# Moving block sums to VectorE and regrouping LN moments, transposes and first-group sums in a fused LayerNorm and graph attention kernel

## The chip, the cores and the metric

The kernel runs on one core of a Trainium2 chip. The metric is the device time of one execution in microseconds (us), the median of several runs. The core has five engines that work side by side, each through its own list of instructions in order: TensorE (in the profile PE, its weight loads PEld), VectorE (DVE), ScalarE (ACT), GpSimd (POOL) and SyncE (SP), which here only starts transfers.

## The reference

x has 128 samples of 128 nodes and 768 features, adj one 128 x 128 matrix for each sample. All is in 32-bit floats.

```
h = max(layernorm(x), 0)                       # over the 768 features
q, k, v = h@Wq + bq, h@Wk + bk, h@Wv + bv      # split into 12 heads of 64
s = q@k^T / 8 + beta * adj;   s = -9e15 where adj == 0
out = x + softmax(s) @ v
```

## The kernel before

Samples are taken in 32 groups of four (NG groups, index G). For each group the normalized input is transposed into six blocks A00 to A12 of 128 x 512 (two sample pairs by three feature blocks). The projections to q, k and v are not done as plain products of blocks: each of three slices of the weights (qk0, v and qk1) is a 3 x 3 arrangement of weight blocks, and a scheme of 15 products of sums of blocks stands in for the 18 products of the plain way. The left factors are the 11 sums of A blocks in SUMS_A (`sum_acts`, called S in the profile) and the right ones the 15 steps of weight sums in SUMS_B (`sum_weights`, T), which are made once, in the first group. The products go into four chains a, b, c and d, each a PSUM bank that TensorE goes on accumulating into; after each product its bank is read out (`product`, L300): the first use of an output goes through an activation on ScalarE or, for v, an add with the bias on VectorE (L325), all later uses are adds on VectorE (L330 for v, L339 for q and k). The next product of a chain has to wait until the bank has been read.

A group goes through slices qk0, v and qk1 in this order (L446 to L490). Between the products of a slice stands other work, listed in `todo` by the number of the product behind which it is written:

- qk0 of group G: the second half of the attention of group G-1, and the loads of x for group G+1.
- v of group G: statistics (`stats`), the mean and variance of group G+1 by two small matmuls (`moments_1`, `moments_2`, PSUM tile pm), its mask (`bias_1`, `bias_2`), and the normalization on ScalarE (`norm`, L256).
- qk1 of group G: the first half of the attention of group G, and the transposes (`to_hT`, L263) and block sums of group G+1.

Attention of a pair of heads is `scores` (matmuls sc, then on VectorE the mask, e, L356, and the exponential on ScalarE, L357) and four products later `attend` (matmuls av, the division on VectorE, the addition to x on GpSimd, xo, L377, and the store). The variance's power -0.5 is on GpSimd (L245).

The first group takes its qk0 slice in the plain way (`plain_slice`), since no weight sums are there yet; `half` normalizes it in two halves, and `after` puts an instruction behind the last transpose and the last GpSimd step of that.

The written order is not quite the order of the engines. A scheduler of the language may move an instruction ahead in its engine's list where nothing that it depends on stands in between; `tc.issue_after(i)` forbids it to stand ahead of instruction i on i's engine. Tiles with `bufs=1` are one buffer: the transposes and sums of group G+1 overwrite those of group G and wait for TensorE's last use of them. The four x tiles of a group are one set of four buffers, so a load of x for the group after next waits for the transposes of the next one.

Before, one in three of the weight sums (n % 3 == 2) and of the activation sums (n % 3 == 1) is on GpSimd, and in the first group all qk0 sums that the choice leaves open:

```
e = e or (nc.gpsimd if n % 3 == 2 else nc.vector)
e.tensor_tensor(wt[sl, name], wt[sl, a], wt[sl, b], ALU.add if sign > 0 else ALU.subtract)
```

Of the kernel before, what the change touches and what calls it, by code (L numbers as in the profile page):

```python
# [104 lines left out]
def direct(ctx, tc, x, adj, wq, bq, wk, bk, wv, bv, beta, out, bad):  # L105
# [82 lines left out]
    def sum_weights(sl, n, e=None):  # L188
        name, a, b, sign = SUMS_B[n]
        if (sl, name) not in wt:  # L190
            raw = [r for r, home in HOME.items() if home == name]
            wt[sl, name] = wt[sl, raw[0]] if raw else const.tile([P, 2, H2], F32, name=f"{sl}_{name}")
        if a[0] == "-":
            nc.vector.scalar_tensor_tensor(wt[sl, name], wt[sl, a[1:]], -1.0, wt[sl, b], op0=ALU.mult,
                                           op1=ALU.add if sign > 0 else ALU.subtract)
        else:
            e = e or (nc.gpsimd if n % 3 == 2 else nc.vector)
            e.tensor_tensor(wt[sl, name], wt[sl, a], wt[sl, b], ALU.add if sign > 0 else ALU.subtract)
# [67 lines left out]
    def sum_acts(G, n):  # L266
        name, a, b, sign = SUMS_A[n]
        t = work.tile([P, 2, H2], F32, tag=name, name=f"{name}_{G}", bufs=1)
        e = nc.gpsimd if n % 3 == 1 else nc.vector
        e.tensor_tensor(t, A[G, a], A[G, b], ALU.add if sign > 0 else ALU.subtract)  # L270
        A[G, name] = t
# [9 lines left out]
    def bias_1(G, raw):  # L281
# [8 lines left out]
        nc.gpsimd.tensor_tensor(a, a, a, ALU.mult)  # L290
# [7 lines left out]
    banks = {}  # L298

    def product(G, sl, n):  # L300
# [15 lines left out]
        for (r, j), sign in uses:  # L316
            key = (G, sl, r, j)
            if sl == "v":
                got = p.rearrange("p g (h d) -> p (g h) d", d=HD)
                if key not in vt:  # L320
# [4 lines left out]
                    nc.vector.tensor_tensor(o4, bias[:, None, :, :].to_broadcast([P, 2, 4, HD]),  # L325
                                            p.rearrange("p g (h d) -> p g h d", d=HD),
                                            ALU.add if sign > 0 else ALU.subtract)
                else:
                    o = vt[key][:, :, 0:HD]
                    nc.vector.tensor_tensor(o, o, got, ALU.add if sign > 0 else ALU.subtract)  # L330
# [6 lines left out]
            else:  # L337
                t = qk[key]
                nc.vector.tensor_tensor(t, t, p, ALU.add if sign > 0 else ALU.subtract)  # L339
# [297 lines left out]
```

## Time and profile before

| | |
|---|---|
| median of 3 runs | 3205.62 us (3204.83 to 3207.76) |
| the profiled execution | 3205.0 us |
| its span, first to last instruction | 3203.1 us |
| mean granted TensorE clock | 0.993 |
| from one V slice to the next, in the middle of the run | 98.05 us |
| first plain slice, from its first matmul | 33.7 us |
| first V slice | 53.04 us |

All views are of one execution. A row of a timeline gives the start, the length, the engine, the line, the operation, what it writes and reads, the count, and in brackets how long the engine was idle before it and what ended that. Rows of one kind that follow one another are merged into one. A row of waits gives the engine that waited, for whom, the total, the count and the longest. A row of stretches gives the stretch, its length and the busy time of each engine in it. Slices in this kernel are read from PE's rows: pc_v with idle or work of another slice ahead is the start of a V slice, pc_qk that of a qk slice.

### The profile page before, as it was taken

To read this page: it belongs to the slowest core of one execution; us is meant where nothing else is said; L and a number is where in the kernel's file an instruction comes from. 1 tells how busy PE (TensorE), PEld (TensorE's weight loads), DVE (VectorE), ACT (ScalarE), POOL (GpSimd) and SP (SyncE) were. 2 spreads that over 40 slices of the span, in tenths; PEclk is the share of its full clock that TensorE was granted. 3 is DMA by queue.
4 is the path that set the end of the run, shared out by engine and by line. 5 is a ranking of instruction groups with operands and counts; after the bars stand their busy time and mean duration, and the time that the engine had idled before them with its cause. 6 is when DMAs were issued, how large, how long until landed. Compare 5 with 4: busy or idle time off the path is not lost.

```text
span 3203.1 us, 46402 instructions
## 1 busy us (share of the span) xinstructions
PE 3115.6 (97%) x17822; PEld 2743.3 (86%) x17822; DVE 1963.9 (61%) x4988; ACT 781.2 (24%) x1665; POOL 590.1 (18%) x489
## 2 busy tenths in 40 slices
PE   5999999999999999999999999999999999999998
PEld 4888888888888888888888888888888888888887
DVE  7665666665565655666655656556666656665554
ACT  1222223222122222232221322222322213222221
POOL 5121111111211111111112111111111111111110
PEclk8999999999999999999999999999999999999998
DMA  5211211111121112212111211112121112121111
GB/s 150 53 50 47 56 54 50 53 47 49 53 60 49 51 43 58 55 50 54 45 52 53 57 50 53 43 55 59 47 56 45 52 53 57 47 57 37 50 40 31
DMA packets 358385, 169.94 MB, mean 53 GB/s; under 512 B 84368, under 2 KB 358032, under 8 KB 358160
## 3 DMA queue, kind: packets, MB, share of 16 engines
q1 hardware_dynamic: 355296, 166.14, 18.9%
q8 instruction: 142, 2.33, 0.3%
q10 hardware_dynamic: 2864, 0.79, 0.1%
q14 instruction: 83, 0.68, 0.1%
HBM read 116.53 MB, written 50.33 MB: 52 GB/s over the span
## 4 chain that ended last, share of the span: by engine, by line
PE 87%; DVE 6%; POOL 3%; issue 2%; ACT 1%; DMA 1%; SPq 1%; ACTq 0%; POOLq 0%; DVEq 0%
PE pc_qk L314 17%; PE pb_qk L314 14%; PE pa_qk L314 14%; PE av L366 10%; PE pd_qk L314 7%; PE sc L353 7%; PE pb_v L314 5%; PE pc_v L314 5%; PE pa_v L314 4%; PE pd_v L314 3%; POOL rstd L245 3%; DVE A L263 2%; DVE v L330 2%; ACT x L256 1%; SPq L180 0%
## 5 line engine op out<-in xcount | busy, mean ns | idle before, releaser
L256 ACT ACTIVATE x<-x,shift,rstd 128x192 f32<-128x192 f32 x512 | 228.0, 533 | 911.7 <-POOL shift L247 911.7
L357 ACT ACTIVATE e<-e 128x512 f32<-128x512 f32 x384 | 235.6, 630 | 821.8 <-DVE e L356 821.8
L377 POOL TENSOR_TENSOR xo<-xo,o 128x512 f32<-128x512 f32 x192 | 244.2, 1272 | 975.0 <-DVE seen L375 590.3
L366 PEld LDWEIGHTS av<-v,e 128*128 128x128 f32 x3072 | 375.6, 193 | 15.4 <-ACT e L357 5.4
L366 PE MATMUL av<-v,e 128*128 128x65 f32 x3072 | 367.2, 273 | 4.7 <-ACT e L357 4.7
L314 PE MATMUL pb_qk<-S,qk_T 128*128 128x256 f32 x1512 | 367.2, 386 | 0.0
L263 DVE STREAM_TRANSPOSE A<-x 128x256 f32<-128x256 f32 x384 | 222.0, 617 | 155.4 <-ACT x L256 120.1
L314 PEld LDWEIGHTS pb_qk<-S,qk_T 128*128 128x128 f32 x1512 | 277.3, 190 | 40.2
L356 DVE SCALAR_TENSOR_TENSOR e<-sc,biasT 128x512 f32<-128x512 f32 x384 | 246.5, 683 | 104.0 <-PE sc L353 103.8
L339 DVE TENSOR_TENSOR qk<-qk,pb_qk 128x512 f32<-128x512 f32 x252 | 171.7, 681 | 175.5 <-PE pb_qk L314 154.5
L335 ACT ACTIVATE qk<-pc_qk,bqk 128x256 f32<-128x256 f32 x378 | 158.3, 470 | 475.4 <-PE pc_qk L314 475.4
L314 PE MATMUL pa_qk<-S,qk_T 128*128 128x256 f32 x1008 | 244.7, 386 | 0.0
L314 PE MATMUL pc_qk<-S,qk_B 128*128 128x256 f32 x1008 | 244.7, 386 | 0.0
L314 PE MATMUL pc_qk<-S,qk_T 128*128 128x256 f32 x1008 | 238.1, 379 | 0.0
L353 PE MATMUL sc<-qk 64*128 64x128 f32 x3072 | 224.4, 285 | 0.0
L314 PEld LDWEIGHTS pc_qk<-S,qk_T 128*128 128x128 f32 x1008 | 191.5, 190 | 26.0
L353 PEld LDWEIGHTS sc<-qk 64*128 64x128 f32 x3072 | 187.1, 188 | 30.1 <-issue 21.2
L314 PEld LDWEIGHTS pc_qk<-S,qk_B 128*128 128x128 f32 x1008 | 186.3, 190 | 30.4
L314 PEld LDWEIGHTS pa_qk<-S,qk_T 128*128 128x128 f32 x1008 | 186.3, 190 | 30.4
L270 POOL TENSOR_TENSOR S<-S,A 128x512 f32<-128x512 f32 x64 | 82.2, 1285 | 630.0 <-PE pa_qk L314 601.1
L339 DVE TENSOR_TENSOR qk<-qk,pd_qk 128x512 f32<-128x512 f32 x126 | 86.6, 687 | 178.1 <-PE pd_qk L314 178.1
L245 POOL TENSOR_TENSOR rstd<-ve,nhalf 128x16 f32<-128x16 f32 (+1 forms) x33 | 93.4, 2830 | 524.6 <-DVE ve L243 524.6
(114 smaller groups left out, 4808.9 us busy)
## 6 DMA issues: line engine op xcount, KB each, us to landing
xo<-in_x_dram SPq DMA_DIRECT2D x192, 256.0 KB, 2.8
out_dram<-xo SPq DMA_DIRECT2D x192, 256.0 KB, 2.2
x<-in_x_dram SPq DMA_DIRECT2D x504, 96.0 KB, 2.2
adj<-in_adj_dram SPq DMA_DIRECT2D x128, 64.0 KB, 2.3
qk_T<-in_L_gnn_Wq_dram SPq DMA_DIRECT2D x10, 128.0 KB, 3.2
qk_T<-in_L_gnn_Wk_dram SPq DMA_DIRECT2D x10, 128.0 KB, 3.3
v_T<-in_L_gnn_Wv_dram SPq DMA_DIRECT2D x5, 256.0 KB, 5.4
qk_B<-in_L_gnn_Wq_dram SPq DMA_DIRECT2D x8, 128.0 KB, 3.4
```

Source lines behind the costliest of these rows:

```text
L245: nc.gpsimd.tensor_tensor(r, ve, nhalf.to_broadcast([P, n]), ALU.pow)
L256: nc.scalar.activation(t, t, AF.Relu, bias=shift[G, n], scale=rstd[G, n])
L263: last = nc.vector.transpose(t[:, :, g * N:(g + 1) * N].rearrange("p c (b i) -> p c b i", i=SQ), src)
L270: e.tensor_tensor(t, A[G, a], A[G, b], ALU.add if sign > 0 else ALU.subtract)
L314: nc.tensor.matmul(p[:, i, :], lhs, rhs, start=(first and i == 0 and c == 0), stop=(c == 1), skip_group_check=True)
L335: nc.scalar.activation(t[:, i, :], p[:, i, :], AF.Identity, bias=bqk[:, i, oc:oc + 1], scale=float(sign))
L339: nc.vector.tensor_tensor(t, t, p, ALU.add if sign > 0 else ALU.subtract)
L353: nc.tensor.matmul(ps[i][:, g, :], t[r, 1, at], t[r, 0, at], start=True, stop=True)
L356: nc.vector.scalar_tensor_tensor(e, ps[i], SCORE_CAP * ISCALE, biasT[G], op0=ALU.min, op1=ALU.add)
L357: nc.scalar.activation(e, e, AF.Exp, scale=1.0 / ISCALE)
L366: nc.tensor.matmul(pa[:, 2 * g + i, :], es[G, oc, i][:, 2 * r + g, :], vt[G, "v", r, h // 4][:, 4 * g + h % 4, :], start=True, stop=True)
L377: nc.gpsimd.tensor_add(t, t, o.rearrange("p a (b j) d -> p (a b) (j d)", j=2))
```

## The change

All block sums go to VectorE, those of weights and those of activations; GpSimd keeps the power, the mask's fill and the addition of x. The mask's square (for a later check of its size) goes from GpSimd to ScalarE. In all groups but the first, statistics of group G+1 are written into the qk0 slice, the moments behind products 1 and 3 of the V slice instead of 5 and 8, and the normalization behind products 6 to 9 instead of 11 to 14; the loads of x are written earlier. The transposes of group G+1 are forbidden to stand ahead of the last V add of group G. In the first group the second half's normalization is written one step earlier; the sums of qk1 and the first mask come into the V slice and must stand behind V's first adds made so far; eight of the qk0 sums follow in the qk1 slice, seven in the next group's qk0 slice.

```
     def sum_weights(sl, n):
...
-            e = e or (nc.gpsimd if n % 3 == 2 else nc.vector)
-            e.tensor_tensor(wt[sl, name], wt[sl, a], wt[sl, b], ALU.add if sign > 0 else ALU.subtract)
+            nc.vector.tensor_tensor(wt[sl, name], wt[sl, a], wt[sl, b], ALU.add if sign > 0 else ALU.subtract)
...
     def sum_acts(G, n):
...
-        e = nc.gpsimd if n % 3 == 1 else nc.vector
-        e.tensor_tensor(t, A[G, a], A[G, b], ALU.add if sign > 0 else ALU.subtract)
+        nc.vector.tensor_tensor(t, A[G, a], A[G, b], ALU.add if sign > 0 else ALU.subtract)
...
     def bias_1(G, raw):
...
-        nc.gpsimd.tensor_tensor(a, a, a, ALU.mult)
+        nc.scalar.activation(a, a, AF.Square)
...
+    def behind_adds(f, *args):
+        with tc.issue_after(added[0].ins):
+            return f(*args)
...
             for g in range(GRP):
-                then(11, lambda g=g: load_x(G + 1, g, (nc.sync,)))
+                then(6, lambda g=g: load_x(G + 1, g, (nc.sync,)))
+                if G:
+                    then(11 + g, lambda g=g: stats(G + 1, g))
...
-            then(3, lambda: half(1, 2))
+            then(2, lambda: half(1, 2))
...
-                then(n // 3 + 13, lambda n=n: after(sum_weights, "qk1", n))
-            then(9, lambda: bias_2(0, after(bias_1, 0, adj_0)))
             plain_slice(0, "qk0", todo)
         else:
+            if G == 1:
+                for n in range(8, len(SUMS_B)):
+                    then(n - 8, lambda n=n: sum_weights("qk0", n))
             slice_of(G, "qk0", todo)
         todo = {}
-        if not G:
-            for n in range(len(SUMS_B)):
-                then(n, lambda n=n: after(sum_weights, "qk0", n, nc.gpsimd))
         if G + 1 < NG:
             got = []
+            at = 1 if G else 6
             for g in range(GRP):
-                then(g, lambda g=g: stats(G + 1, g))
-                then(11 + g, lambda g=g: norm(G + 1, g))
-            then(5, lambda: got.extend(moments_1(G + 1, 0, GRP * NB)))
-            then(7, lambda: got.append(bias_1(G + 1, load_adj(G + 1))))
-            then(8, lambda: moments_2(G + 1, 0, GRP * NB, *got[:2]))
-            then(11, lambda: bias_2(G + 1, got[2]))
+                if not G:
+                    then(g, lambda g=g: stats(G + 1, g))
+                then(at + 5 + g, lambda g=g: norm(G + 1, g))
+            then(at, lambda: got.extend(moments_1(G + 1, 0, GRP * NB)))
+            then(at + 2, lambda: moments_2(G + 1, 0, GRP * NB, *got[:2]))
+            if G:
+                then(8, lambda: got.append(bias_1(G + 1, load_adj(G + 1))))
+                then(12, lambda: bias_2(G + 1, got[2]))
+            else:
+                for n in range(len(SUMS_B)):
+                    then(n, lambda n=n: behind_adds(sum_weights, "qk1", n))
+                then(10, lambda: bias_2(0, behind_adds(bias_1, 0, adj_0)))
         slice_of(G, "v", todo)
         todo = attention(G, 0)
+
+        def transposes(n):
+            with tc.issue_after(added[G].ins):
+                to_hT(G + 1, int(n[1]), int(n[2]))
+
+        if not G:
+            for n in range(8):
+                then(n, lambda n=n: behind_adds(sum_weights, "qk0", n))
+            then(13, lambda: bias_2(1, bias_1(1, load_adj(1))))
         if G + 1 < NG:
             for n, at in HT_AT.items():
-                then(at, lambda n=n: to_hT(G + 1, int(n[1]), int(n[2])))
+                then(at, lambda n=n: transposes(n))
```

`added[G]` is the last add of a product's bank that has been written for group G (in `product`, all three kinds of adds on VectorE set it).

How the instructions stand on the engines is shown at three places. First VectorE at the end of a V slice, that of group 8, before. In the names v0 to v6 are tiles of v, pa_8_v the bank of chain a in the V slice of group 8, and A01_9 a block of group 9.

```order
L330 TENSOR_TENSOR v1_109<-v1_109,pc_8_v_5783 128x8x64
L263 STREAM_TRANSPOSE A01_9_5937<-x_9_0_5721 128x2x128
L263 STREAM_TRANSPOSE A00_9_5966<-x_9_0_5721 128x2x128
L330 TENSOR_TENSOR v4_112<-v4_112,pa_8_v_5794 128x8x64
L263 STREAM_TRANSPOSE A02_9_5985<-x_9_0_5721 128x2x128
L263 STREAM_TRANSPOSE A01_9_5937<-x_9_1_5726 128x2x128
L263 STREAM_TRANSPOSE A00_9_5966<-x_9_1_5726 128x2x128
L330 TENSOR_TENSOR v1_109<-v1_109,pb_8_v_5804 128x8x64
```

The same place in the changed kernel:

```order
L328 TENSOR_TENSOR v1_109<-v1_109,pc_8_v_5800 128x8x64
L328 TENSOR_TENSOR v4_112<-v4_112,pa_8_v_5806 128x8x64
L328 TENSOR_TENSOR v1_109<-v1_109,pb_8_v_5820 128x8x64
L328 TENSOR_TENSOR v3_111<-v3_111,pc_8_v_5800 128x8x64
L328 TENSOR_TENSOR v2_110<-v2_110,pa_8_v_5806 128x8x64
L328 TENSOR_TENSOR v6_114<-v6_114,pb_8_v_5820 128x8x64
L262 STREAM_TRANSPOSE A01_9_5937<-x_9_0_5651 128x2x128
L262 STREAM_TRANSPOSE A01_9_5937<-x_9_1_5656 128x2x128
```

The transposes of group 9 stood among the last adds of V; they now stand behind all of them, and the adds follow one another.

Second VectorE in the first group, at the first adds of its V slice (v0 and v1 with the bias bv_b), before. qk1_T and qk0_T are weight sums of slices qk1 and qk0, and st_1 the statistics of group 1; eight more sums of qk1 stand ahead of the first row.

```order
L198 TENSOR_TENSOR qk1_T13_234<-qk1_T13_234,qk1_B01_231 128x512
L198 TENSOR_TENSOR qk1_T1_462<-qk1_T1_462,qk1_B21_237 128x512
L198 TENSOR_TENSOR qk1_T4_228<-qk1_T10_225,qk1_T4_228 128x512
L194 SCALAR_TENSOR_TENSOR qk0_T9_488<-qk0_B01_131,qk0_B12_143 128x512
L218 BN_STATS st_1_490<-x_1_0_396 128x6 x3
L325 TENSOR_TENSOR v0_108<-bv_b_155,pc_0_v_482 128x8x64
```

The same place in the changed kernel:

```order
L268 TENSOR_TENSOR S11_0_436<-A11_0_300,A01_0_216 128x512
L197 TENSOR_TENSOR qk0_T13_134<-qk0_T13_134,qk0_B01_131 128x512
L217 BN_STATS st_1_455<-x_1_0_333 128x6 x4
L323 TENSOR_TENSOR v0_108<-bv_b_155,pc_0_v_449 128x8x64
L194 SCALAR_TENSOR_TENSOR qk1_T9_460<-qk1_B01_231,qk1_B12_243 128x512
L217 BN_STATS st_1_455<-x_1_1_338 128x6 x2
L323 TENSOR_TENSOR v1_109<-bv_b_155,pa_0_v_462 128x8x64
```

The sums of qk1 stood ahead of the first add; they now begin behind it and lie between the adds. From the first S to that add stand 27 sums, those of the activations and of the V weights and one of qk0.

Third VectorE in the qk1 slice of group 8, around the second pair of e, before. sm, rs, seen and o are the division of `attend`, sc_8_1 the scores of the second pair of heads, S3_9, S6_9 and S8_9 sums for group 9.

```order
L372 TENSOR_TENSOR o_8_0_6007<-av_8_0_1_6020,rs_8_0_1_6027 128x256
L375 TENSOR_TENSOR seen_104<-seen_104,rs_8_0_1_6027 128x4
L356 SCALAR_TENSOR_TENSOR e_8_1_0_6046<-sc_8_1_0_6036,biasT_8_5203 128x512
L356 SCALAR_TENSOR_TENSOR e_8_1_1_6049<-sc_8_1_1_6037,biasT_8_5203 128x512
L270 TENSOR_TENSOR S3_9_6077<-A00_9_5966,A01_9_5937 128x512
```

The same place in the changed kernel:

```order
L370 TENSOR_TENSOR o_8_0_6007<-av_8_0_1_6020,rs_8_0_1_6027 128x256
L373 TENSOR_TENSOR seen_104<-seen_104,sm_8_0_1_6025 128x4
L373 TENSOR_TENSOR seen_104<-seen_104,rs_8_0_1_6027 128x4
L268 TENSOR_TENSOR S8_9_6063<-A10_9_5997,A11_9_5975 128x512
L354 SCALAR_TENSOR_TENSOR e_8_1_0_6046<-sc_8_1_0_6036,biasT_8_5228 128x512
L354 SCALAR_TENSOR_TENSOR e_8_1_1_6049<-sc_8_1_1_6037,biasT_8_5228 128x512
L268 TENSOR_TENSOR S6_9_6070<-S2_9_6061,A02_9_5985 128x512
```

Before, the first e of this pair followed straight on the rows of `attend`; now the sum S8 stands between, and S6, which was on GpSimd, follows.

More of the change, by code (lines that the diff above doesn't have):

```diff
@@ L296, in bias_2 @@
         nc.vector.tensor_tensor(seen_b, seen_b, bm, ALU.max)
-    banks = {}
+    banks, added = {}, {}
     def product(G, sl, n):
@@ L324, in product @@
                     bias = bv_b[:, j * 2 * P:(j + 1) * 2 * P].rearrange("p (h d) -> p h d", d=HD)
-                    nc.vector.tensor_tensor(o4, bias[:, None, :, :].to_broadcast([P, 2, 4, HD]),
-                                            p.rearrange("p g (h d) -> p g h d", d=HD),
-                                            ALU.add if sign > 0 else ALU.subtract)
+                    added[G] = nc.vector.tensor_tensor(o4, bias[:, None, :, :].to_broadcast([P, 2, 4, HD]),
+                                                        p.rearrange("p g (h d) -> p g h d", d=HD),
+                                                        ALU.add if sign > 0 else ALU.subtract)
                 else:
                     o = vt[key][:, :, 0:HD]
-                    nc.vector.tensor_tensor(o, o, got, ALU.add if sign > 0 else ALU.subtract)
+                    added[G] = nc.vector.tensor_tensor(o, o, got, ALU.add if sign > 0 else ALU.subtract)
             elif key not in qk:
@@ L338, in product @@
                 t = qk[key]
-                nc.vector.tensor_tensor(t, t, p, ALU.add if sign > 0 else ALU.subtract)
+                added[G] = nc.vector.tensor_tensor(t, t, p, ALU.add if sign > 0 else ALU.subtract)
     es, xo = {}, {}
```

2 lines of the change are left out of this document (1 added, 1 removed).

## The prediction

> **What bounds the kernel now.** I read the page first, then PE's own waits, then the busy time by stretches, then the timelines around each wait. The page's first part says that PE is busy nearly throughout.
>
> ```profile
> PE 3115.6 (97%) x17822; PEld 2743.3 (86%) x17822; DVE 1963.9 (61%) x4988; ACT 781.2 (24%) x1665; POOL 590.1 (18%) x489
> ```
>
> So only a PE wait, or a longer PE, changes the time. The waits of PE, longest in total first (us in total, times, longest):
>
> ```profile
> PE pa_v L314 <- DVE v L330: 29.6, 31, 1.0
> PE pc_v L314 <- DVE v L325: 23.5, 1, 23.5
> ```
>
> One wait comes back in 31 groups, one comes once; both are in the V slice, and both are for VectorE to empty a PSUM bank. The stretches (length, then busy time of PE, PEld, DVE, ACT, POOL, then the clock): the first group's V slice, then V, qk1 and the following qk0 slice of the middle of the run, and the last group's V slice, which prepares no next group.
>
> ```profile
> 50.62:103.66 53.04, 28.68 (x125) 24.11 (x124) 45.77 (x69) 7.96 (x18) 27.38 (x18) 0.77 0.08 20
> ...
> 1644.41:1672.42 28.01, 26.88 (x125) 23.08 (x124) 14.89 (x29) 7.12 (x16) 4.06 (x3) 1.00 0.13 35
> 1672.42:1707.44 35.02, 35.02 (x217) 31.14 (x216) 26.39 (x71) 8.63 (x18) 6.35 (x5) 1.00 0.22 64
> 1707.44:1742.46 35.02, 35.02 (x218) 31.14 (x217) 19.05 (x56) 8.63 (x18) 6.88 (x7) 1.00 0.20 53
> 3115.07:3140.97 25.90, 25.90 (x122) 22.80 (x121) 10.90 (x16) 0.00 (x0) 0.94 (x1) 1.00 0.07 21
> ```
>
> The qk slices have PE busy for all of their 35.02 us: nothing is to be had there, only lost. A V slice takes 25.90 us when nothing else is asked of it (15 products of 1.727) and 28.01 with a next group. Part of those 2.11 us are the two small matmuls of the LN moments:
>
> ```profile
> 1654.77 0.31 PE L227 MATMUL pm<-st,mean 128*128 128x32 f32 x2
> 1654.91 1.97 PE L314 MATMUL pc_v<-v_B,S 128*128 128x256 f32 x8
> 1656.72 0.59 PE L314 MATMUL pb_v<-v_T,S 128*128 128x256 f32 x2
> ```
>
> From 1654.77 to 1656.72 are 1.95 us for a pair that would take 1.727 without the small one: 0.22 each, 0.45 for two. The other 1.66 are at the end of the slice:
>
> ```profile
> 1665.58 1.89 PE L314 MATMUL pc_v<-v_T,A 128*128 128x256 f32 x8
> 1668.42 1.99 PE L314 MATMUL pa_v<-v_B,S 128*128 128x256 f32 x8 [0.95 <-DVE v L330]
> 1670.59 1.99 PE L314 MATMUL pb_v<-v_T,S 128*128 128x256 f32 x8 [0.17 <-DVE v L330]
> 1672.42 0.38 PE L314 MATMUL pc_qk<-S,qk_T 128*128 128x256 f32 x1
> ```
>
> Start to start these three products take 2.84, 2.17 and 1.83 us where 1.727 is the rule, so 1.66 are lost, more than the 0.95 and 0.17 named as waits, since the weight loads start late too. VectorE shows why:
>
> ```profile
> 1662.33 0.69 DVE L330 TENSOR_TENSOR v<-v,pc_v 128x512 f32<-128x512 f32 x1 [0.95 <-PE pc_v L314]
> 1666.65 1.15 DVE L263 STREAM_TRANSPOSE A<-x 128x256 f32<-128x256 f32 x2 [3.63 <-ACT x L256]
> 1667.73 0.64 DVE L330 TENSOR_TENSOR v<-v,pa_v 128x512 f32<-128x512 f32 x1
> ```
>
> VectorE stands 3.63 us at a transpose whose input ScalarE has not normalized yet, and the add that PE waits for is queued behind it. The transpose is late because its chain starts late: the power on GpSimd, then the norms on ScalarE.
>
> ```profile
> 1661.52 2.90 POOL L245 TENSOR_TENSOR rstd<-ve,nhalf 128x16 f32<-128x16 f32 x1 [16.17 <-DVE ve L243]
> 1664.50 0.22 POOL L247 TENSOR_TENSOR shift<-mean,rstd 128x16 f32<-128x16 f32 x1
> ```
>
> ```profile
> 1664.76 7.12 ACT L256 ACTIVATE x<-x,shift,rstd 128x192 f32<-128x192 f32 x16 [28.74 <-POOL shift L247]
> ```
>
> **The steady groups.** The second moment matmul moves from behind the ninth product to behind the fourth, five products or 8.6 us earlier; the norms then end at 1664.76 + 7.12 - 8.6 = 1663.3, nine microseconds ahead of the slice's end, and no transpose stands ahead of an add any more. The four small moment instructions and the adds between which they now stand have 1 us of idle VectorE at each product (the 0.95 in the add's row), so the adds stay on time. Gain: 1.66 in each of groups 1 to 30, 49.8 us. The two moment matmuls stay, 0.45.
>
> What is added falls on the qk1 slice. Eight transposes of 0.57 (the 1.15 for two) come over from the V slice, four block sums of activations come over from GpSimd at 0.6 to 0.68, one V add fewer spills in. VectorE's 26.39 us become about 26.4 + 4.6 + 2.7 - 0.7 = 33.0 of 35.02. That is nearly full, so each deadline of PE there counts. The tightest is the bank of chain c, which ScalarE empties behind the second pair of exponentials:
>
> ```profile
> 1686.76 0.15 DVE L375 TENSOR_TENSOR seen<-seen,rs 128x4 f32<-128x4 f32 x1
> 1686.92 1.28 POOL L377 TENSOR_TENSOR xo<-xo,o 128x512 f32<-128x512 f32 x1 [1.33 <-DVE seen L375]
> ...
> 1687.09 1.29 DVE L356 SCALAR_TENSOR_TENSOR e<-sc,biasT 128x512 f32<-128x512 f32 x2 [0.18 <-PE sc L353]
> 1687.88 1.22 ACT L357 ACTIVATE e<-e 128x512 f32<-128x512 f32 x2 [2.76 <-DVE e L356]
> ...
> 1689.02 0.84 ACT L335 ACTIVATE qk<-pc_qk,bqk 128x256 f32<-128x256 f32 x2
> ...
> 1692.27 0.38 PE L314 MATMUL pc_qk<-S,qk_B 128*128 128x256 f32 x1
> ```
>
> From e's start to the end of that eviction are 2.77 us, and PE wants the bank 19.85 us into the slice: e must start by 17.08. Before, it starts at 14.67 (1687.09 less 1672.42). Before, the attention rows end at 14.5 (1686.76 + 0.15). In the new order VectorE reaches them no later than their matmuls end, but takes the second matmul's row ahead of the first one's work, so I have them end at 14.9; then comes the sum S8, and e starts at 15.5. If S8 meets GpSimd's xo add, which starts in the same instant and takes 1.28, e starts at 16.75. Either way the bank is free in time, by 1.6 or by 0.3 us. I take no stall, and keep 0 to 0.7 us a group for the range.
>
> The Trainium skill, "GPSIMD Engine Reference", Key points, says that GpSimd and VectorE share their SBUF interfaces and that VectorE instructions with two SBUF inputs contend; by it S8 meets the add and e does not, which would put e at 16.75. The trace agrees as to kind: sums of two SBUF tensors take 1.75 beside GpSimd and 0.68 without it (rows below), while e, with one input in PSUM, keeps 1.29 for two beside the xo add.
>
> The loads of x for the group after next wait for the later transposes, and SyncE's queue holds them behind the stores of xo; their statistics stand on VectorE at the slice's end, ahead of adds that have several microseconds of slack. Price 0, up to about 0.5 a group. The squares of the mask move from GpSimd to ScalarE, at about the 0.61 of an exponential, at the end of the qk0 slice; VectorE has 16 idle us there. Price 0.
>
> **The first group.** The 23.45 us are VectorE's too:
>
> ```profile
> 54.07 1.89 PE L314 MATMUL pb_v<-v_T,S 128*128 128x256 f32 x8
> 79.42 3.53 PE L314 MATMUL pc_v<-v_T,S 128*128 128x256 f32 x8 [23.45 <-DVE v L325]
> ```
>
> ```profile
> 34.27 4.58 DVE L270 TENSOR_TENSOR S<-A,A 128x512 f32<-128x512 f32 x3
> ...
> 75.55 1.75 DVE L198 TENSOR_TENSOR qk_T<-qk_T,qk_T 128x512 f32<-128x512 f32 x1
> 77.21 0.68 DVE L194 SCALAR_TENSOR_TENSOR qk_T<-qk_B,qk_B 128x512 f32<-128x512 f32 x1
> 77.81 0.87 DVE L218 BATCH_NORM_STATS2 st<-x 128x6 f32<-128x192 f32 x3
> 78.60 0.66 DVE L325 TENSOR_TENSOR v<-bv_b,pc_v 128x512 f32<-128x512 f32 x1
> ```
>
> Its sums begin at 34.27, most of them take 1.75, and the first V add stands behind the sums of qk1 at 78.60. Afterwards 27 sums stand ahead of that add; with GpSimd quiet they follow one another in 0.60 (77.21 to 77.81), 16.3 us, so from 34.3 at the latest they end at 50.6, and four statistics later, at 51.7, VectorE waits for the first product, which ends at 52.4. The sums of qk1 now lie between the adds: 15 sums, 16 adds, 12 statistics, the mask and the moments are about 26 us for a slice of 26.35. The slice should take 26.4 to 27: gain 26.0 to 26.7.
>
> Part of it is given back in the first qk1 slice. The first mask's square stands on ScalarE behind the next group's norms: second moment matmul at about 67, its values at 68.6, then 2.90 + 0.22 + 7.12 and the square, 79.6. VectorE's maximum over it waits so long, and everything behind is late: from there to the second e stand eight weight sums, ten transposes, the second mask, the first e, three adds, the attention rows and S9, some 18.1 us. That e starts at 97.7, the bank of c is free at 100.5, and PE, with the slice begun at 77.3, wants it at 97.2: a stall of 3.3 us, 4.5 if S9 meets the xo add. From 0 (the maximum not so late) to 9 (the 15 sums of 0.6 paid after all) is the range; I take 3.9.
>
> After the long wait the eight passes take 3.53 us instead of 1.73, and the clock of that stretch is 0.77. The Trainium skill, "TensorE: Matmul & The Clock Gate", Part 1, says that an idle window of about 3.4 us halves PE's clock until it was busy as long again; by it a stall of 3.3 to 4.5 may cost these 1.8 us once more. No run shows a stall of that length yet. The waits of 0.95 leave the clock at 1.00. Between no restart and one of the 1.80 that the rows show (3.53 less 1.73) I take the half, 0.9.
>
> **The sum.** The profiled execution took 3205.0 us (span 3203.1). 3205.0 - 49.8 - 26.4 + 3.9 + 0.9 = 3133.6; the median of the runs shown lies 0.6 above the profiled time, so 3134. The floor, with no stall anywhere, is 3205.0 - 49.8 - 26.7 = 3128.5.
>
> **Rivals.**
> *VectorE overfull in qk1.* 33.0 us, and three collisions with an xo add of up to 1.2 each, are 36.6 in a slice of 35.02. For it: the margin of 0.3 above. Against: statistics and late sums can slide into the qk0 slice, where VectorE is busy for 19.05 of 35.02. If 0.3 to 1.2 us a group reach PE, 9 to 36 us come back: 3143 to 3170, most likely about 3155.
> *The V wait stays*, because another row of VectorE or ScalarE is late in its place. Only the first group's 22 us are gained: 3183. Against: with the transposes gone, nothing in the slice but small moment rows stands among the adds.
> *Slower.* The same bank of c: if e in qk1 starts later than 19.5 instead of 15.5, each group loses over 2.4 us, more than the V slice and the first group give. That takes two xo-sized holdups beyond the one I count; at 20.0 the stall is 2.9, and 30 x (2.9 - 1.66) less 22 is 15 slower: 3220.
> *Nothing changes.* VectorE's new stalls eat just what the V slice gave; a coincidence of sizes.
>
> **How the numbers follow.** A measurement of this kernel can tell about 0.2% from no change, 6 us. Forecast 0.64 (3128 to 3143), VectorE overfull 0.25, V wait stays 0.06, nothing 0.02, slower 0.03. Faster by over 0.2%: 0.64 + 0.25 + 0.06 = 0.95. The range from 3127 to 3162 holds the forecast and about two thirds of the first rival.
>
> **What would show it.** Right: V slices of 26.4 us, no PE wait for DVE v there, qk1 slices still of 35.02 with VectorE busy for about 33, the first V slice under 28. Wrong: PE waits for ACT qk or DVE qk in qk1 in every group, or slices over 35.1; PE waits for pa_v still listed 30 times; a granted clock below 1.00 outside the start and the first qk1 slice.

## The result and the profile after

The changed kernel takes 3132.4 us (median of 4 runs, 3132.07 to 3136.48) where the kernel before took 3205.3 on the same chip (4 runs): a ratio of 0.9774, 95% interval 0.9757 to 0.9791. The forecast was 3134. Five later runs gave 3132.64 (3132.41 to 3132.87).

The first part of the page after: VectorE has taken on GpSimd's work, and PE is busy for 99% of a span of 3130.3 us.

```profile
PE 3099.0 (99%) x17822; PEld 2748.1 (88%) x17822; DVE 1999.5 (64%) x5137; ACT 800.6 (26%) x1697; POOL 378.0 (12%) x308
```

PE's waits after (for whom, total, times, longest). Both waits for DVE v are gone; one new wait comes once, in the first group. The three waits for e are the tail, the last group's attention, when no product is left to lie between.

```profile
PE av L364 <- ACT e L355: 4.7, 3, 1.7
PE pc_qk L312 <- ACT qk L333: 2.7, 1, 2.7
```

The stretches after: the first V slice, the start of the first qk1 slice, then V, qk1 and the following qk0 slice of the middle of the run (length, busy time of PE, PEld, DVE, ACT, POOL, clock).

```profile
50.47:76.83 26.36, 26.36 (x126) 23.16 (x124) 22.83 (x50) 6.15 (x15) 3.34 (x2) 1.00 0.07 11
76.83:113.00 36.17, 33.44 (x193) 28.98 (x192) 33.69 (x76) 11.12 (x25) 3.07 (x2) 0.95 0.29 73
1597.27:1623.62 26.35, 26.35 (x126) 23.25 (x125) 11.88 (x22) 7.12 (x16) 4.06 (x3) 1.00 0.07 21
1623.62:1658.64 35.02, 35.02 (x218) 31.14 (x217) 29.85 (x80) 8.61 (x18) 3.07 (x2) 1.00 0.27 76
1658.64:1693.65 35.01, 35.01 (x217) 31.13 (x216) 20.40 (x59) 9.27 (x19) 4.62 (x5) 1.00 0.21 53
```

V slices went from 28.01 to 26.35, 30 times; the first one from 53.04 to 26.36; the qk slices are where they were, but for the first qk1 and the qk0 slice behind it, which took 74.72 us together in place of 70.04. That is the whole account: 3203.1 - 30 x 1.66 - 26.7 + 4.7 = 3131.3, and of the last 1.0 a start 0.15 earlier and an end that comes 0.7 sooner behind the last V slice (61.4 us in place of 62.1) are most, the rest roundings.

VectorE's timeline at the end of a V slice: ahead of the last add VectorE is idle for 1.04 us until PE is done, as it is ahead of the adds before it, so none is late, and the transposes come behind it.

```profile
1623.82 0.69 DVE L328 TENSOR_TENSOR v<-v,pb_v 128x512 f32<-128x512 f32 x1 [1.04 <-PE pb_v L312]
1624.42 2.20 DVE L262 STREAM_TRANSPOSE A<-x 128x256 f32<-128x256 f32 x4
```

The place of the tightest deadline, in the qk1 slice that starts at 1623.62: on VectorE the sum S8 and the second pair of e, on GpSimd the addition to x, on ScalarE the exponentials and the eviction of chain c's bank.

```profile
1638.37 0.69 DVE L268 TENSOR_TENSOR S<-A,A 128x512 f32<-128x512 f32 x1
1638.97 1.28 DVE L354 SCALAR_TENSOR_TENSOR e<-sc,biasT 128x512 f32<-128x512 f32 x2
```

```profile
1638.39 1.79 POOL L375 TENSOR_TENSOR xo<-xo,o 128x512 f32<-128x512 f32 x1 [29.44 <-DVE o L370]
```

```profile
1639.75 1.23 ACT L355 ACTIVATE e<-e 128x512 f32<-128x512 f32 x2 [3.44 <-DVE e L354]
1640.88 0.82 ACT L333 ACTIVATE qk<-pc_qk,bqk 128x256 f32<-128x256 f32 x2
```

The second e starts 15.35 us into the slice, and the bank is free at 18.08, 1.77 ahead of PE's 19.85. S8 does meet GpSimd's addition, but it is GpSimd that stands: 1.79 where the addition takes 1.27 or 1.28 alone.

The first group, VectorE: the first V add, the maximum over the first mask's square, the second e.

```profile
52.40 0.69 DVE L323 TENSOR_TENSOR v<-bv_b,pc_v 128x512 f32<-128x512 f32 x1 [2.71 <-PE pc_v L312]
...
79.19 0.69 DVE L293 TENSOR_REDUCE bm<-adjT 128x4 f32<-128x512 f32 x1 [2.85 <-ACT adjT L288]
...
96.85 1.28 DVE L354 SCALAR_TENSOR_TENSOR e<-sc,biasT 128x512 f32<-128x512 f32 x2
```

And PE there. The eight passes behind the wait take 3.52 us, start to start, in place of 1.73; behind them PE is at its full pace again.

```profile
99.57 3.68 PE L312 MATMUL pc_qk<-S,qk_B 128*128 128x256 f32 x8 [2.73 <-ACT qk L333]
103.09 1.90 PE L364 MATMUL av<-v,e 128*128 128x65 f32 x16
```

### The profile page after: what moved, and what is told of

Same layout as the page of the kernel before. It is cut to its first block, busy times and chain, and to the rows that moved or that the text cites. A ratio compares the mean times of both kernels' runs of the same rounds, so it can differ in the third digit from the quotient of the medians.

```text
span 3130.3 us, 46295 instructions
## 1 busy us (share of the span) xinstructions
PE 3099.0 (99%) x17822; PEld 2748.1 (88%) x17822; DVE 1999.5 (64%) x5137; ACT 800.6 (26%) x1697; POOL 378.0 (12%) x308
## 4 chain that ended last, share of the span: by engine, by line
PE 98%; DVE 1%; ACT 0%; DMA 0%; issue 0%; POOL 0%; DVEq 0%; ACTq 0%
PE pc_qk L312 18%; PE pb_qk L312 14%; PE pa_qk L312 14%; PE av L364 11%; PE pc_v L312 9%; PE pb_v L312 7%; PE pa_v L312 7%; PE pd_qk L312 7%; PE sc L351 7%; PE pd_v L312 4%; PE plain L402 1%; ACT x L255 0%; DMA x<-in_x_dram 0%; DVE A L262 0%; PE pm L226 0%; PE pm L239 0%
## 5 line engine op out<-in xcount | busy, mean ns | idle before, releaser
L375 POOL TENSOR_TENSOR xo<-xo,o 128x512 f32<-128x512 f32 x192 | 261.1, 1360 | 2455.5 <-DVE seen L373 1539.2
L312 PE MATMUL pb_v<-v_T,S 128*128 128x256 f32 x768 | 184.2, 382 | 0.0
L370 DVE TENSOR_TENSOR o<-av,rs 128x256 f32<-128x256 f32 x384 | 160.2, 418 | 2.1 <-DVE seen L373 0.4
```

The source lines that it names most:

```text
L312: nc.tensor.matmul(p[:, i, :], lhs, rhs, start=(first and i == 0 and c == 0), stop=(c == 1), skip_group_check=True)
L370: nc.vector.tensor_mul(o[:, r], pa[:, :, 0:HD], rs.to_broadcast([P, 4, HD]))
L375: nc.gpsimd.tensor_add(t, t, o.rearrange("p a (b j) d -> p (a b) (j d)", j=2))
```

## The experiments

The change has three parts: all sums on VectorE, a new order of the steady groups, a new order of the first. The theory that the prediction stands on: a transpose that waits for the norms is what made PE lose 1.66 us in each steady V slice, and sums beside GpSimd's sums plus their place ahead of the adds made the first V slice long. The rivals: GpSimd's sums slow VectorE everywhere, so that their move is the gain; the transposes' own time among the adds is the loss; VectorE has no room left in qk1.

**All sums on VectorE, and nothing else** (kernel before, written order kept):

```
-            e = e or (nc.gpsimd if n % 3 == 2 else nc.vector)
-            e.tensor_tensor(wt[sl, name], ...)
+            nc.vector.tensor_tensor(wt[sl, name], ...)
...
-        e = nc.gpsimd if n % 3 == 1 else nc.vector
-        e.tensor_tensor(t, A[G, a], A[G, b], ...)
+        nc.vector.tensor_tensor(t, A[G, a], A[G, b], ...)
...
-    then(n, lambda n=n: after(sum_weights, "qk0", n, nc.gpsimd))
+    then(n, lambda n=n: after(sum_weights, "qk0", n))
```

> The kernel before, with every block sum on VectorE and nothing else changed: order, moments, transposes and the mask's square stay. Theory (the steady loss is a transpose that waits for the norms, whoever does the sums): the steady V slices stay at 28.01 us; only the first group gains, since its sums follow one another in 0.60 us where they took 1.65 beside GpSimd: first V add at about 62 in place of 78.6, the 23.45 us wait shrinks to 6 or 7; 15 more sums on VectorE in that slice give 2 to 4 back. About 3189 us (3185 to 3193). Rival (VectorE is slowed by GpSimd's sums everywhere, so that quiet on GpSimd is what gained): V slices near 26.4 and a time near 3140.

3190.19 us (ratio 0.9951, 0.9934 to 0.9967), as the theory had it. The stretches of this run, first V slice and a steady one:

```profile
50.40:86.85 36.45, 31.22 (x145) 26.38 (x144) 36.45 (x76) 2.41 (x6) 4.56 (x3) 0.95 0.10 23
1627.40:1655.40 28.00, 26.85 (x126) 23.05 (x125) 14.48 (x30) 7.09 (x16) 4.40 (x3) 1.00 0.12 33
```

The steady slice has not moved; the first one is 16.6 us shorter, and the first V add is at 61.72, PE's wait for it 4.99. The scheduler changed PE's list in the first group, though: one product and some score matmuls of the qk1 slice stand in the V slice (145 matmuls in place of 125), and behind it PE waits 2.09 us for the bank of chain c. The three slices of the first group from V on are 16.6 us shorter together too (106.45 in place of 123.07).

**The steady order alone** (kernel before, sums and first group as they were):

```
-                then(11, lambda g=g: load_x(G + 1, g, (nc.sync,)))
+                then(6 if G else 11, lambda g=g: load_x(G + 1, g, (nc.sync,)))
+                if G:
+                    then(11 + g, lambda g=g: stats(G + 1, g))
...
+                then((6 if G else 11) + g, lambda g=g: norm(G + 1, g))
+            then(1 if G else 5, lambda: got.extend(moments_1(G + 1, 0, GRP * NB)))
+            then(8 if G else 7, lambda: got.append(bias_1(G + 1, load_adj(G + 1))))
+            then(3 if G else 8, lambda: moments_2(G + 1, 0, GRP * NB, *got[:2]))
+            then(12 if G else 11, lambda: bias_2(G + 1, got[2]))
...
+        def transposes(n):
+            if not G:
+                return to_hT(G + 1, int(n[1]), int(n[2]))
+            with tc.issue_after(added[G].ins):
+                to_hT(G + 1, int(n[1]), int(n[2]))
```

> The kernel before, with only the new order of groups 1 to 30 (moments behind the products 1 and 3, loads of x and statistics earlier, transposes behind the last V add); a third of the sums stay on GpSimd, the square too, and the first group is as before. Theory: all of the steady gain comes, 30 x 1.66 = 49.8, V slices 26.35, the first group's wait of 23.45 stays: 3155 to 3157 us. Rival (the sums' move is what matters): V slices stay near 28 and the time near 3200. Second rival (GpSimd's sums slow VectorE in the fuller qk1 slice): V slices 26.35, but qk1 slices over 35.02 with a wait for ACT qk, 9 to 36 us back.

3157.3 us (ratio 0.9846, 0.9829 to 0.9862). The first V slice keeps its 53.31. A steady V slice and the qk1 slice behind it:

```profile
1620.19:1646.54 26.35, 26.35 (x125) 23.25 (x124) 11.88 (x22) 7.12 (x16) 4.07 (x3) 1.00 0.07 21
1646.54:1681.56 35.02, 35.02 (x218) 31.14 (x217) 30.32 (x77) 8.61 (x18) 6.85 (x5) 1.00 0.27 76
```

All of the steady gain is here, with GpSimd's sums still in the qk1 slice (POOL busy for 6.85). Moving those sums to VectorE is worth nothing in the steady groups, and does no harm.

**Which half of the steady order?** First the changed kernel without the tie of the transposes:

```
     def transposes(n):
-        with tc.issue_after(added[G].ins):
-            to_hT(G + 1, int(n[1]), int(n[2]))
+        if not G:
+            with tc.issue_after(added[G].ins):
+                return to_hT(G + 1, int(n[1]), int(n[2]))
+        to_hT(G + 1, int(n[1]), int(n[2]))
```

> The changed kernel, with the transposes of groups 1 to 30 no longer tied behind the last V add; the moments stay early. Eight transposes go back into the V slice. Theory (what cost was the wait for the norms): the norms are done 7 us ahead of the slice's end, so the transposes wait for nothing and fit in the 1.04 us of idle VectorE at each product: V slices 26.35 to 26.5, 3132 to 3137 us. Rival (the transposes' own 0.57 us among the adds is what cost): V slices 27 to 28, 3150 to 3182 us.

3185.79 us (ratio 0.9937, 0.992 to 0.9954): all 50 us of the steady V slices are lost again (the profiled execution is 53 us longer than the changed kernel's, 3 of them at the start and in the tail), so the theory's expectation was wrong. VectorE, GpSimd and PE in a V slice that starts at 1622.99:

```profile
1636.60 1.16 DVE L262 STREAM_TRANSPOSE A<-x 128x256 f32<-128x256 f32 x2 [3.04 <-ACT x L255]
1637.69 0.64 DVE L323 TENSOR_TENSOR v<-bv_b,pa_v 128x512 f32<-128x512 f32 x1
```

```profile
1631.47 2.90 POOL L244 TENSOR_TENSOR rstd<-ve,nhalf 128x16 f32<-128x16 f32 x1 [7.54 <-DVE ve L242]
```

```profile
1637.25 1.89 PE L312 MATMUL pd_v<-v_T,A 128*128 128x256 f32 x8
1640.53 1.99 PE L312 MATMUL pc_v<-v_B,S 128*128 128x256 f32 x8 [1.39 <-DVE v L323]
```

The earlier norms did not free the transposes: the scheduler, which orders the engines' lists when the program is built, put the transposes just as much earlier. They end their wait 5.13 us behind the start of the power on GpSimd (1636.60 less 1631.47), exactly as before (1666.65 less 1661.52), and the slice takes the same 28.00. VectorE's stall has only moved five products (8.6 us) ahead.

Then the changed kernel with the tie, and the moments at their old places:

```
-            at = 1 if G else 6
+            at = 5 if G else 6
...
-                then(at + 5 + g, lambda g=g: norm(G + 1, g))
+                then(11 + g, lambda g=g: norm(G + 1, g))
...
-            then(at + 2, lambda: moments_2(G + 1, 0, GRP * NB, *got[:2]))
+            then(8, lambda: moments_2(G + 1, 0, GRP * NB, *got[:2]))
```

> The changed kernel, with the moments of groups 1 to 30 back at the places they had before (behind the products 5 and 8, norms from 11 on); the transposes stay behind the last V add. Theory: the add waits for no transpose, so the V slice stays 26.35; the norms end about 1 us into the qk1 slice, the transposes there wait up to 1 us, and the bank of chain c has 1.77 us in hand: 3132 to 3136 us. Rival (the early moments are what the gain needs, a late transpose is only moved): VectorE is late in qk1 and PE waits there for ACT qk, 0.5 to 1.7 us a group: 3148 to 3182 us.

3134.27 us (3132.01 to 3137.26; ratio 0.9779, 0.9763 to 0.9796), its span 3130.2 as the changed kernel's 3130.3. ScalarE's norms now begin late and end 1.1 us behind the start of the qk1 slice at 1623.13, and it costs nothing, since VectorE first transposes the samples that are ready:

```profile
1617.13 7.13 ACT L255 ACTIVATE x<-x,shift,rstd 128x192 f32<-128x192 f32 x16 [27.43 <-POOL shift L246]
```

```profile
1623.93 2.21 DVE L262 STREAM_TRANSPOSE A<-x 128x256 f32<-128x256 f32 x4
```

So without the tie there is no steady gain, and with it the early moments are not needed. The earlier loads and statistics stood in every run that had the gain; whether it needs them was not tested.

**Is it the wait, or the transposes among the adds?** The run without the tie could not tell. This one ties them behind an earlier add, by which the norms are done:

```
+                    if n < 11:
+                        tie[G] = added[G]
...
-            with tc.issue_after(added[G].ins):
+            with tc.issue_after((tie if G else added)[G].ins):
```

> The changed kernel, with the transposes of groups 1 to 30 tied behind the V add of product 10 in place of the last one: all eight go back into the V slice, four, three and one of them ahead of the last three adds. The moments stay early, so the norms are done by then. Theory (what cost PE was VectorE standing still for the norms, not the transposes' own time): nothing waits, the adds come at most 1.3 us later than now, PE's next banks have about 2 us in hand: V slices 26.35, 3131 to 3135 us. Rival (any transpose ahead of an add costs): V slices 27 to 28, 3150 to 3182 us.

3137.75 us (3136.75 to 3139.01; ratio 0.9786, 0.9771 to 0.9801). VectorE at the end of a V slice that lasts from 1601.38 to 1627.73:

```profile
1621.63 2.17 DVE L262 STREAM_TRANSPOSE A<-x 128x256 f32<-128x256 f32 x4
1623.72 0.65 DVE L328 TENSOR_TENSOR v<-v,pb_v 128x512 f32<-128x512 f32 x1
1624.29 1.66 DVE L262 STREAM_TRANSPOSE A<-x 128x256 f32<-128x256 f32 x3
```

All eight transposes stand among the last adds, wait for nothing, and the slice takes 26.35. So it was the wait, not the place. The expected 3131 to 3135 us were missed by what lies elsewhere. The profiled execution is 6.6 us longer than the changed kernel's: the first qk1 and qk0 slices take 79.27 where they take 74.5 to 74.7 in the changed kernel, behind the same wait of 2.72 (last section), and the tail, which is what follows the last V slice, takes 2.7 more.

**The first group's order with GpSimd's sums** (changed kernel, a third of the sums back on GpSimd):

```
-            nc.vector.tensor_tensor(wt[sl, name], ...)
+            (nc.gpsimd if n % 3 == 2 else nc.vector).tensor_tensor(wt[sl, name], ...)
...
-        nc.vector.tensor_tensor(t, A[G, a], A[G, b], ...)
+        (nc.gpsimd if n % 3 == 1 else nc.vector).tensor_tensor(t, A[G, a], A[G, b], ...)
```

> The changed kernel, with a third of the sums back on GpSimd as before; order, tie and square as changed. Theory: in groups 1 to 30 nothing (four sums of some 1.3 us each on GpSimd, VectorE's beside them slower, but the bank of chain c has 1.77 us in hand): qk slices 35.02. In the first group 17 sums on VectorE go at about 1.65 while GpSimd does its 9 and at 0.60 after that: first V add at about 54.3 in place of 52.4, and the V slice, with five sums on GpSimd beside ten on VectorE, some 2 to 8 us longer: 3135 to 3142 us. Rival (GpSimd's sums delay VectorE's e in the fuller qk1 slice): PE waits for ACT qk in each group, 3150 us or more.

3142.36 us (3135.3 to 3143.14; ratio 0.9802, 0.9787 to 0.9817). The profiled run is the fastest of the four, with a mean clock of 0.997; the others have 0.994 and are some 7 us longer, which fits a longer stay at half clock behind the wait (last section) but wasn't traced. In the profile the steady slices are 26.35 and 35.02, the first V add is at 54.10, the first V slice takes 27.83, and the wait in the first qk1 slice is 4.10 in place of 2.73. VectorE and GpSimd side by side:

```profile
38.19 0.68 DVE L197 TENSOR_TENSOR v_T<-v_B,v_T 128x512 f32<-128x512 f32 x1
38.79 1.75 DVE L268 TENSOR_TENSOR S<-A,A 128x512 f32<-128x512 f32 x1
40.47 1.75 DVE L194 SCALAR_TENSOR_TENSOR v_T<-v_B,v_B 128x512 f32<-128x512 f32 x1
```

```profile
38.34 1.65 POOL L268 TENSOR_TENSOR S<-S,A 128x512 f32<-128x512 f32 x1 [1.23 <-DVE S L268]
39.95 3.39 POOL L197 TENSOR_TENSOR v_T<-v_T,v_B 128x512 f32<-128x512 f32 x2
```

Of the first V slice's 26.7 us, the sums' move alone brought 16.6 and the order alone 25.2 (53.04 less 27.83): the two overlap, and the order is the larger. What each part of that order is worth (the sums of qk1 behind the adds, the second half's normalization a step earlier, the mask's place) was not taken apart. In the first qk1 slice the sums' move is worth 1.4 us of wait more.

**Mending the first group.** The maximum at 79.19 waits for a square that stands on ScalarE behind the norms. First the mask earlier:

```
-                then(10, lambda: bias_2(0, behind_adds(bias_1, 0, adj_0)))
+                then(7, lambda: bias_2(0, behind_adds(bias_1, 0, adj_0)))
```

> The changed kernel, with the first group's mask made behind product 7 of the first V slice in place of product 10, so that its square goes ahead of most norms on ScalarE. Theory (the maximum over the square, 2.85 us behind the norms, is what makes the second e late and PE idle): the maximum waits for nothing, the second e starts at about 94.2 in place of 96.85, the wait of 2.73 and the clock's restart go: 4.7 us less than the changed kernel, 3127 to 3129 us. Rival (VectorE is simply overfull in the first group: 15 sums, ten transposes and two masks): e stays behind 96, at most 1 us is gained, 3131 to 3133.

3133.23 us (3132.2 to 3133.39; ratio 0.9772, 0.9759 to 0.9785) beside 3132.64 of the changed kernel on the same chip:

> The changed kernel once more, beside the run with the mask made earlier: 3132 to 3133 us, first qk1 and qk0 slices together 74.7 us.

The theory missed. What the rival foresaw came about, nothing gained and the second e at 97.14, but not for its reason, as the next run shows: the square still stood behind three norms, so the maximum waited 3.23 us, now in the middle of the V adds:

```profile
74.72 0.69 DVE L293 TENSOR_REDUCE bm<-adjT 128x4 f32<-128x512 f32 x1 [3.23 <-ACT adjT L288]
```

```profile
76.06 1.99 PE L312 MATMUL pa_v<-v_B,S 128*128 128x256 f32 x8 [1.82 <-DVE v L328]
...
99.86 1.99 PE L312 MATMUL pc_qk<-S,qk_B 128*128 128x256 f32 x8 [0.24 <-ACT qk L333]
```

The V slice took 28.44, the qk slices 70.54: the loss moved from one slice to the other, 2.6 us in place of 4.5, and a tail 1.8 us longer and a start 0.7 later took the difference.

Then the first mask's square on VectorE itself:

```
-        nc.scalar.activation(a, a, AF.Square)
+        if G:
+            nc.scalar.activation(a, a, AF.Square)
+        else:
+            nc.vector.tensor_tensor(a, a, a, ALU.mult)
```

> The changed kernel, with the first group's square alone on VectorE (0.60 us) in place of ScalarE; order otherwise kept. Theory: the maximum no longer waits 2.85 us behind the norms, the square costs 0.60, so the second e starts at about 94.6 in place of 96.85 and the bank of chain c is free at 97.3: PE waits 0.4 us in place of 2.73, too short to halve the clock: 4.2 us less than the changed kernel, 3128 to 3129 us, faster than both. Rival (VectorE's queue is late anyway): e behind 96, PE waits 2 us or more, 3131 to 3133 us.

3131.49 us (3127.48 to 3131.81; ratio 0.9765, 0.9752 to 0.9778). In the first group all is as the theory had it (the rival, with e behind 96, is out, though the median lies in its range):

```profile
77.21 0.69 DVE L296 TENSOR_REDUCE bm<-adjT 128x4 f32<-128x512 f32 x1
...
94.64 1.28 DVE L357 SCALAR_TENSOR_TENSOR e<-sc,biasT 128x512 f32<-128x512 f32 x2
```

The slices there take 70.40, PE's wait no longer shows, and the last V slice ends at 3064.92 where it ended at 3068.66 in the second profile of the changed kernel (taken on another chip, with a time before that is within 0.2 us). Yet only 1.1 us arrive at the median. The tail takes the rest: from the end of the last V slice to the last matmul it takes 58.7 us here and 55.6 there. Two stretches of it, in this run and then in the changed kernel's, with the clock in the third column from the right. PE's first wait in the tail ends at 3102.69 here and at 3106.43 there; here the clock falls right behind it, there it is still at 1.00:

```profile
3100.00:3105.00 5.00, 3.50 (x31) 3.10 (x31) 1.98 (x3) 1.23 (x2) 0.88 (x1) 0.87 0.29 86
3105.00:3110.00 5.00, 3.49 (x22) 3.08 (x22) 2.87 (x12) 1.07 (x2) 1.26 (x1) 0.50 0.08 22
```

```profile
3100.00:3105.00 5.00, 4.93 (x42) 4.23 (x40) 2.99 (x13) 0.00 (x0) 1.27 (x1) 1.00 0.00 0
3105.00:3110.00 5.00, 3.43 (x32) 2.98 (x32) 2.61 (x11) 1.23 (x2) 0.00 (x0) 1.00 0.38 108
```

One of the five runs took 3127.48 us, 3 to 4 us less than the others; that fits a tail of the shorter kind, but it was not traced. This version has the lowest median of all, but its interval overlaps that of the changed kernel (0.9758 to 0.9784 in its five later runs): that it is faster is shown for the first group, not for the whole.

**Is VectorE full in qk1?** Three runs compute the first e of the second pair k + 1 times in groups 1 to 30 (k = 2, 4, 7), at 0.60 us for each repeat:

```
+            for _ in range(k if G in range(1, NG - 1) and oc == 1 and not i else 0):
+                nc.vector.scalar_tensor_tensor(e, ps[i], SCORE_CAP * ISCALE, biasT[G], ...)
             nc.vector.scalar_tensor_tensor(e, ps[i], SCORE_CAP * ISCALE, biasT[G], ...)
```

> The changed kernel, with the first e of the second pair in the qk1 slice of groups 1 to 30 computed three times over on VectorE, 2 x 0.64 = 1.29 us more ahead of the bank of chain c. Theory (a deadline: the bank is free 1.77 us before PE wants it): no PE wait, qk1 slice 35.02, 3132 to 3134 us. Rival (VectorE has no room left in qk1: its work is the bound): 1.29 us a group come through, 39 us, about 3171.

> As the run before, but five times over: 4 x 0.64 = 2.58 us more. Theory: 2.58 less 1.77 is a wait of 0.8 us for ACT qk in each of 30 groups, 24 us: 3156 to 3158 us, clock at 1.00 (idle of 0.95 us left it there). Rival (VectorE is the bound): 2.58 a group, 3210 us.

> As the run before, but eight times over: 7 x 0.64 = 4.51 us more. Theory: a wait of 2.74 us in each of 30 groups, 82 us; each is about as long as the wait in the first group, after which PE ran at half clock for 3.5 us in one profile and for 13 us in another, so 1.8 to 6.6 us more each time: 3268 to 3410 us. Rival (the clock's loss belongs to the first group alone): 82 us and no more, 3214 us, clock at 1.00.

3133.31 (3132.03 to 3137.02; ratio 0.9773, 0.9758 to 0.9788), 3137.72 (3137.47 to 3139.07; 0.9789, 0.9774 to 0.9804) and 3136.99 (3136.81 to 3143.79; 0.9793, 0.9778 to 0.9808). The rival is out: 4.2 us more of VectorE's work in each group leave the slices nearly as they are. The last run's qk1 and qk0 slices:

```profile
1625.45:1660.60 35.15, 35.15 (x218) 31.06 (x217) 30.52 (x75) 8.64 (x18) 3.40 (x3) 1.00 0.27 74
1660.60:1695.62 35.02, 35.02 (x218) 31.14 (x217) 23.41 (x70) 9.27 (x19) 4.83 (x5) 1.00 0.21 55
```

What stands behind e on VectorE slid on into the next slice (23.41 there, 20.40 in the changed kernel). The pair takes 70.17 us in place of 70.03, 4 us in 30 groups; in the run with four more e it is 70.11, 2 us, and a tail of 58.6 us in place of 55.4 makes the rest. But the theory's waits did not come either, because the experiment did not test what it was to test. ScalarE in the last run, in the slice that starts at 1625.45:

```profile
1642.46 0.63 ACT L357 ACTIVATE e<-e 128x512 f32<-128x512 f32 x1 [4.31 <-DVE e L356]
1642.99 0.82 ACT L333 ACTIVATE qk<-pc_qk,bqk 128x256 f32<-128x256 f32 x2
1649.82 0.63 ACT L357 ACTIVATE e<-e 128x512 f32<-128x512 f32 x1 [6.01 <-DVE e L356]
```

With the longer e the scheduler put the eviction of chain c's bank ahead of the second exponential in all three runs, so no eviction stood behind the delay. It also put sums and adds between the repeats, and in the run with seven of them PE's matmuls av of this pair two products later. Whether a second e behind 17.08 us would make PE wait in the steady groups stays open; the first group, where the eviction does stand behind both, is the one place that shows it (e 2.7 us ahead of the bank, PE waiting 2.73).

## Why the prediction was right, step by step

- **Steady V slices.** Predicted 1.66 in each of 30, measured 28.01 to 26.35. The cause was right: VectorE standing for the norms with an add queued behind. The credit was not. The step gave both edits as reasons, the norms "nine microseconds ahead of the slice's end" and the transposes away from the adds. Without the tie the early norms gain nothing; with it they are not needed. (They end 7.5 us ahead of the slice's end, since the slice is itself 1.66 shorter.)
- **The two small matmuls stay.** They do: 26.35 in place of the last group's 25.90.
- **qk1.** The slice stayed at 35.02 and the second e came at 15.35, predicted 15.5. VectorE's load was mis-sized: 29.85 us where the step had 26.4 + 4.6 + 2.7 - 0.7 = 33.0. The term that failed is the 2.7 for the four sums from GpSimd. The run with the new order and GpSimd's sums has 30.32, which is the step without that term; with the sums on VectorE it is 29.85. One of the four slid into the qk0 slice, three add 0.60 each, and the same three on GpSimd had held VectorE up by more: beside them, three of its rows take 0.90, 1.15 and 1.44 us in that run where 0.13, 0.15 and 0.69 are the rule, 2.5 together. The case "VectorE overfull", at a quarter the largest rival, was therefore given too much: 4.2 us more of VectorE's work came in with 0.13 us more for the pair of slices.
- **The collision of S8.** It happens, but the price falls on GpSimd's addition (1.79), not on VectorE, so the 16.75 worked out for it did not come.
- **Loads, statistics, squares at 0.** No PE wait for any of them in the steady groups.
- **First V slice.** Predicted 26.4 to 27, measured 26.36; its first add predicted at 52.4, measured at 52.40.
- **First qk1 slice.** The maximum at 79.6 was 79.19 (with its wait of 2.85), e at 97.7 was 96.85, the stall of 3.3, taken at 3.9 for the sum, was 2.73. The square on VectorE shows that the maximum was the cause: e goes to 94.64 and the wait is gone. The half restart of the clock, 0.9, was a whole one, 1.8. Together 4.7 against 4.8: one term 1.2 too large, the other 0.9 too small, so that the sum came out is luck.

## What to carry to other kernels

A stall of an in-order engine is mended where the queue is, by putting what waits behind what others wait for; starting its inputs earlier helps only if the scheduler leaves it where it was. Sort a several-part change by stage before crediting its parts: here the tie of the transposes brought 50 us that the early norms without it did not, the first group's order most of the rest, and the move of the sums off GpSimd, the part that the change is named after, nothing in steady state. Where a gain of a few microseconds is looked for, look also at what it does to the clock at the end: a shorter middle was followed by a longer tail in one run here.

## What the runs showed of the hardware

A wait of 2.73 us halves PE's clock, and how long it stays so differs. One of 2.09, in the run with all sums on VectorE and nothing else, did not: the product behind it takes 1.83 us, start to start.

```profile
93.18 1.99 PE L312 MATMUL pc_qk<-S,qk_T 128*128 128x256 f32 x8 [2.09 <-ACT qk L333]
95.01 1.89 PE L312 MATMUL pd_qk<-S,qk_B 128*128 128x256 f32 x8
```

In the changed kernel the half clock was over with the eight passes behind the wait, and in seven more profiles with a wait of 2.71 to 4.10 us it cost 1.5 to 1.8 us too. In the run with the transposes tied behind the tenth product's add, behind the same wait, PE stayed at half for about 13 us (start to start 3.6, 3.4 and 2.0 us where 1.7, 1.8 and 1.1 are the rule; the product at 108.15 takes twice its 1.89, the ones from 113.67 on are back at it):

```profile
99.12 3.78 PE L312 MATMUL pc_qk<-S,qk_B 128*128 128x256 f32 x8 [2.72 <-ACT qk L335]
102.70 3.52 PE L366 MATMUL av<-v,e 128*128 128x65 f32 x16
106.14 2.08 PE L353 MATMUL sc<-qk 64*128 64x128 f32 x16
108.15 3.78 PE L312 MATMUL pa_qk<-S,qk_T 128*128 128x256 f32 x8
```

PE had no wait behind the first of these rows, so it is not idleness behind the first wait that kept the clock low; what decides between 3.5 and 13 us was not settled. The Trainium skill, "TensorE: Matmul & The Clock Gate", Part 1, gives an idle window of about 3.4 us as what halves the clock and as long a busy one as what restores it; here 2.73 are enough for the one, and for the other the run above needs nearly four times that. The tail shows the first point too: three waits of 1.5 to 1.7 us within 13 to 16 us halve the clock, sometimes behind the first of them and sometimes behind the second, and its length up to the last matmul lies between 55.3 and 58.8 us over all profiles for the same work. Whether the kernel or the single execution decides which it is was not settled. Changes of 3 us in this kernel are to be read from its slices, not from its total.

VectorE and GpSimd hold each other up when both work on sums of two SBUF tensors. Side by side each gets one sum done in about 1.67 us (38.79 to 40.47 in the run with a third of the sums on GpSimd), so two in 1.67; VectorE alone does two in 1.20 (0.60 for one, 77.21 to 77.81 in the kernel before), GpSimd alone takes 1.27 for one. With a third of the sums on GpSimd the first V add came at 54.10 in place of 52.40. It looks like taking turns, the first to start going first: in the steady qk1 slice S8 starts at 1638.37 and keeps its 0.69, and the addition, started 0.02 later, takes 0.52 more. The Trainium skill, "SBUF — State Buffer", "SBUF: two separate sides", says that the pair of ports that the two engines share is an exclusive lock, held for the whole instruction by whichever starts first; these rows agree.
